# Row maxima of attention scores from half the keys and the difference of the halves, in a kernel that overlaps attention with a scan

## The chip, the core and the metric

The kernel runs on one core of one Trainium2 chip. Its engines work at the same time, each through its own queue in program order: TensorE (PE; matmuls, its weight loads are PEld), VectorE (DVE), ScalarE (ACT), GpSimd (POOL) and SyncE (SP, which issues the DMAs). The metric is the device time of one execution in microseconds; less is better.

## What is computed

Two layers for 16 images of 256 channels and 32 x 32 pixels, seen as 1024 tokens. The first is a transformer block with 4 heads of 32, the second a gated state-space scan over the tokens with 512 inner channels and 64 states. Cut to what matters here:

```python
# layer 0, after a group norm
q, k, v = (qkv[:, :, 0], qkv[:, :, 1], qkv[:, :, 2])
dots = jnp.einsum('bihd,bjhd->bhij', q, k) * scale
attn = jax.nn.softmax(dots, axis=-1)
out = jnp.einsum('bhij,bjhd->bihd', attn, v)
# layer 1, after another group norm
def step(h, inp):
    d_t, B_t, C_t, u_t = inp
    dA = jnp.exp(d_t[..., None] * A)
    h = dA * h + (d_t * u_t)[..., None] * B_t[:, None, :]
    y = jnp.einsum('bdn,bn->bd', h, C_t)
    return (h, y)
```

A softmax is the same whatever is subtracted from a row before the exponential. The kernel subtracts the row's maximum over all 1024 keys, and gets it in a pass of its own.

## The kernel before

**Units and side work.** The scan over one image takes 256 units, one per pair of inner channels (128 partitions are 64 states times 2 channels, the free dimension the 1024 tokens). For unit n the main loop writes, in this order:

- `load(n + 6)` on SP: the channel's input `dub`, 512 KB, into one of 7 buffers; `inputs(n + 4)` on POOL: times B (L911)
- the next part of `outputs` of the eight units before: 32 matmul records into `yb` (L953); ACT copies them off on every second unit (L959); once in eight units 64 more, `turn` (L965), with a copy (L969)
- `scan(n)` on DVE (L928); it needs the decays of unit n and `dub`
- `decay(n + 2)`: two matmuls spread the step sizes into an `a` tile of two banks (L920), an Exp on ACT (L922). There are two `a` tiles, so this waits until `scan(n)` has read its own
- a step of the side work: image b+1's norms, attention and scan inputs, image b-1's gate and store. These are generators; each `yield` gives a share, a share of 1 or more is at least one unit, and the shares are stretched so that the side work of one image fills its 256 units. The number and place of the yields set which unit a step falls in.

A dependency added at the end holds each engine to the program's order. For image 0 the side work runs before the scan starts, alone.

**The row maxima (L412 to L446).** `q4` and `k4` hold the four heads on 32 partitions each. The pass goes over 16 blocks of 64 queries (`c`) and, within each, over the two halves of the keys (`hf`): 32 steps, one yield each. A step computes the scores of four heads against 512 keys: tile `g` of two takes heads 2g and 2g+1, one above the other (`e`), and fills one PSUM bank. The matmul contracts over the head's 32 partitions, so the four heads of a step stand in four row groups of the array. fp32 matmuls stand in the trace as two records each. `maxima()`, at the head of the next step, reduces both tiles over the keys on DVE into one column of `mx` each (L417). At the end `neg` takes the maximum over the two halves and the negative (L446); a transposing matmul and DMAs put it as a 33rd row under the queries, and the later score matmuls then give scores minus maximum.

**PSUM.** Eight banks: `a` has four (`aps`), `yb` one, `accp` one (the attention sums `av`), `mm` two. Beside the scan `psum()` gives the `mm` banks in turn, and `psum3()` goes round `mm, mm, accp`. In the part that runs alone both take from `mm` and the idle `a` tiles through `free_bank`, which hands out an `a` tile in two halves and keeps the second in the list `spare`.

**SBUF tiles the change uses.** `half` (`hwork`): four buffers of 128 x 512 fp32, used by the norms. `ptp` (tag `pt`): four of the same size, used after this pass for the exponentials and for the scan's step sizes.

Of the kernel before, what the change touches and what calls it, by code (L numbers as in the profile page):

```python
# [11 lines left out]
F32 = mybir.dt.float32  # L12
BF16 = mybir.dt.bfloat16
AF = mybir.ActivationFunctionType
ALU = mybir.AluOpType
AX = mybir.AxisListType
# [3 lines left out]
P = 128  # L20
# [3 lines left out]
HL = 512  # L24
NG = 16
HEADS, DH = 4, 32
INNER = HEADS * DH
NJ = L // P
# [22 lines left out]
def attention_then_scan_kernel(  # L51
# [18 lines left out]
    nc = tc.nc  # L70
    B = x.shape[0]

    def pool(name, bufs, **kw):
        return ctx.enter_context(tc.tile_pool(name=name, bufs=bufs, **kw))
# [5 lines left out]
    ptp = pool("ptp", 4)  # L80
    small = pool("small", 2)
# [12 lines left out]
    alone, spare = cycle((mm, aps)), []  # L94

    def bank(src, name):
        return src.tile([P, HL], F32, name=name, tag="mm" if src is mm else "av")

    def free_bank(name):
        if spare:  # L100
            return spare.pop()
        if next(alone) is mm:
            return bank(mm, name)
        both = aps.tile([P, L], F32, name=name, tag="a")
        spare.append(both[:, hs(1)])
        return both[:, hs(0)]

    def psum(name, dims=P):
        return (bank(mm, name) if beside["scan"] else free_bank(name))[:dims]
# [4 lines left out]
    def psum3(name):  # L114
        return bank(next(three), name) if beside["scan"] else free_bank(name)

    def work(name, n=L):
        return wide.tile([P, L + 2 + CONV], F32, name=name, tag="wide")[:, :n]

    def hwork(name):  # L120
        return half.tile([P, HL], F32, name=name, tag="half")

    def hs(h):
        return ts(h, HL)
# [37 lines left out]
    for k in range(ND):  # L162
# [4 lines left out]
        for j in range(2):  # L167
# [3 lines left out]
                start=(j == 0), stop=(j == 1),  # L171
# [195 lines left out]
    def attention_layer(b):  # L367
# [23 lines left out]
        q4, k4 = work("q4"), work("k4")  # L391
# [17 lines left out]

        mx = small.tile([P, 2, 2 * NJ, 2], F32, name="mx", tag="mx")  # L412
        waiting = []

        def maxima():
            for s, g, c, hf in waiting:
                nc.vector.tensor_reduce(mx[:, g, c, hf : hf + 1], s, AX.X, ALU.max)  # L417
            waiting.clear()

        def against(pair, e):  # L420
# [3 lines left out]
        to_space = [  # L424
            partial(spaced, to, src, pair)
            for pair in range(HEADS // 2) for to, src in ((qas, q4), (kas, k4))
        ] + [partial(against, pair, e) for pair in range(HEADS // 2) for e in range(2)]
        for c in range(2 * NJ):
            for hf in range(2):
                maxima()  # L430
                for g in range(2):
                    waiting.append((psum("s_ps"), g, c, hf))
                for h in range(HEADS):
                    g, e = divmod(h, 2)
                    r = ts(h, DH)
                    nc.tensor.matmul(  # L436
                        waiting[g][0][ts(e, 64)], q4[r, ts(c, 64)], k4[r, hs(hf)],
                        start=True, stop=True,
                    )
                if to_space:  # L440
                    to_space.pop(0)()
                yield 1
        maxima()
        del q4, k4, to_space
        neg = small.tile([P, HEADS * NJ], F32, name="neg", tag="neg")
        nc.vector.tensor_reduce(neg, mx.rearrange("p g c k -> p (g c) k"), AX.X, ALU.max, negate=True)  # L446
        ps = psum("neg_ps", HEADS * NJ)[:, :P]
        nc.tensor.matmul(ps, neg, ident, start=True, stop=True)
        yield 1
# [2 lines left out]
        for h in range(HEADS):  # L452
            pair, e = divmod(h, 2)
# [6 lines left out]
        for g in range(2):  # L460
# [3 lines left out]
            for j in range(NJ // 2):  # L464
                for k in range(KC):
                    nc.tensor.matmul(
                        ps[:, j, :], xn[k][:, ts(g * (NJ // 2) + j, P)], wv_s[:, k, :],
                        start=(k == 0), stop=(k == KC - 1),
# [14 lines left out]
        for pair in range(HEADS // 2):  # L483
# [3 lines left out]
            for hf in range(2):  # L487
# [11 lines left out]
                for j in range(NJ):  # L499
                    scores = []  # L500
                    for e in range(2):
                        r = ds(2 * DH * e, DH + 1)
                        s = psum("st_ps")
# [6 lines left out]
                    for s in scores:  # L510
                        pt = ptp.tile([P, HL], F32, name="pt", tag="pt")
# [376 lines left out]
    def load(n):  # L888
        b, k, q, e, i = units[n]
        st = state[b]  # L890
        if (k, q, e, i) == (0, 0, 0, 0):
            bt = hst.tile([P, L], F32, name="bt", tag="bt")
            ct = hst.tile([P, L], F32, name="ct", tag="ct")
            for v, lo in ((bt, 0), (ct, NS)):
                src = st["rows"][lo : lo + NS, :]
                nc.sync.dma_start(v, src.unsqueeze(1).to_broadcast([NS, 2, L]))
            blocks[b] = {"bt": bt, "ct": ct}
        if i == 0:
            pieces = blk.tile([P, HL], BF16, name="pieces", tag="pieces")
            rows = ds(((k * 4 + q) * 2 + e) * 48, 48)  # L900
            for hf in range(2):
                nc.sync.dma_start(pieces[ds(64 * hf, 48)], st["dps"][rows, hs(hf)])
            blocks[b, k, q, e] = pieces
        du = dutp.tile([P, L], F32, name="dub", tag="dub")
        src = st["dus"][ts(k, P)].rearrange("(q j i e) c -> q e i j c", q=4, j=2, i=SLOTS)[q, e, i]
        nc.sync.dma_start(du, src.unsqueeze(0).to_broadcast([NS, 2, L]))
        loaded[n] = du
# [70 lines left out]
    def prepare(b):  # L978
        return chain(first_norm(b), attention_layer(b), scan_inputs(b))
# [15 lines left out]

    AHEAD, LEAD = 6, 4
    beside["scan"] = True
    for n in range(AHEAD):
        load(n)
    for n in range(LEAD):  # L1000
# [5 lines left out]
    for n, (b, k, q, e, i) in enumerate(units):  # L1006
        at = n % UNITS
        if at == 0:
            parts = [prepare(b + 1)] if b + 1 < B else []
            total = steps * len(parts)  # L1010
            if b > 0:
                if b + 1 < B:
                    parts = [
                        first_norm(b + 1, gate_loads(b - 1)), gate_and_store(b - 1),
                        attention_layer(b + 1), scan_inputs(b + 1),
                    ]
                else:
                    parts = [gate_and_store(b - 1)]
                total = total + GATE
            side = chain(*parts)  # L1020
            rate, due = rate_for(total, UNITS - AHEAD - 3), 0.0
# [102 lines left out]
```

## Time and profile before

| | |
|---|---|
| median of 3 runs | 12974.16 us (12973.16 to 13009.8) |
| the profiled execution | 12999.14 us, span 12997.4 us |
| mean granted TensorE clock | 0.799 |
| scan, L928 | 4096 instructions, 9217.0 us busy, 2280 ns each |
| row maxima, L417 | 1023 instructions, 657.5 us busy, 698 ns each |
| score matmuls of that pass, L436 | 4092 records, 823.4 us busy, 617 ns each |
| Exp of the decays, L922 | 4096 instructions, 4463.0 us busy, 1090 ns each |
| the scan's inputs on POOL, L911 | 4096 instructions, 9781.6 us busy, 2410 ns each |

How to read it: the page gives busy time, share of the span and number of instructions of each engine, then groups of instructions: line, engine, operation, tiles written and read, shapes, count, then busy time and mean length of one, then the idle time of the engine just before them and what ended it. The timeline lists instructions in order of time: start, length, engine, line, operation, count. Lengths overlap a little where one instruction starts before the one ahead has drained, so the space an instruction takes in its queue is read from start to start. PEclk is the granted share of the full TensorE clock.

### The profile page before, as it was taken

The page shows a single profiled execution, that of the slowest core. Times are in us where ns is not written, and L with a number is a line of the kernel's source. Part 1 is how long each engine was busy: PE and PEld are TensorE (multiplying, and loading weights), DVE is VectorE, ACT ScalarE, POOL GpSimd, SP SyncE. Part 2 cuts the span into 40 slices and gives each one's busy share as a digit, 9 for nine tenths or more (in the row PEclk, how much of TensorE's full clock was granted, in tenths as well). Part 3 has the DMA queues.
Part 4 walks back from the last instruction along what each step waited for, and adds up shares of the span by engine and source line. Part 5 has one row for each costly group of instructions (what it writes and reads, how often), then busy time and mean ns, then how long its engine had stood idle before and what let it go on. Part 6 is the DMA issues. An engine that isn't in the chain of part 4 may idle for free.

```text
span 12997.4 us, 424123 instructions
## 1 busy us (share of the span) xinstructions
PE 9794.6 (75%) x186800; PEld 5486.9 (42%) x186800; DVE 11576.5 (89%) x7464; ACT 7531.4 (58%) x10421; POOL 10007.5 (77%) x4201
## 2 busy tenths in 40 slices
PE   6676877868778687786878768687786877868777
PEld 2344444444444444444444434444344444444445
DVE  3789999899999899898999999999998998989998
ACT  2465664656646566565665656656565664656654
POOL 0588877878778787787878878787787877878798
PEclk8887977878778797887879878797787978868755
DMA  1467666675666766667666666766667666676676
GB/s 51 166 218 245 206 215 224 221 243 203 212 224 220 241 204 214 230 217 239 207 228 224 217 231 211 241 210 215 225 220 241 209 215 224 224 239 202 224 252 229
DMA packets 1038400, 2820.09 MB, mean 217 GB/s; under 512 B 290370, under 2 KB 368451, under 8 KB 1036548
## 3 DMA queue, kind: packets, MB, share of 16 engines
q1 hardware_dynamic: 1036548, 2792.97, 63.2%
q8 instruction: 1459, 23.90, 0.7%
q14 instruction: 393, 3.22, 0.1%
HBM read 2513.82 MB, written 261.62 MB: 214 GB/s over the span
## 4 chain that ended last, share of the span: by engine, by line
DVE 37%; PE 29%; issue 13%; ACT 10%; DMA 7%; POOL 3%; SPq 1%; DVEq 0%; POOLq 0%; ACTq 0%
DVE h L928 26%; PE yb L953 5%; DVE mx L417 5%; ACT a L922 5%; PE a L920 4%; DMA dub<-dus 4%; PE av L492 3%; POOL dub L911 2%; PE st_ps L504 2%; PE z_ps L640 2%; PE g_ps L689 2%; PE yb L965 1%; PE m_ps L865 1%; DMA xs<-ud 1%; DVE u L675 1%
## 5 line engine op out<-in xcount | busy, mean ns | idle before, releaser
L911 POOL TENSOR_TENSOR dub<-dub,bt 128x1024 f32<-128x1024 f32 x4096 | 9781.6, 2410 | 2841.4 <-DMA dub<-dus 2555.3
L928 DVE TENSOR_TENSOR_SCAN h<-a,dub 128x1024 f32<-128x1024 f32 x4096 | 9217.0, 2280 | 798.1 <-ACT a L922 492.2
L922 ACT ACTIVATE a<-a,acol 128x1024 f32<-128x1024 f32 x4096 | 4463.0, 1090 | 3177.0 <-PE a L920 3112.4
L920 PE MATMUL a<-pieces,pick 48*128 48x512 bf16 x8192 | 1915.4, 458 | 2380.2 <-DVE h L928 2258.4
L953 PEld LDWEIGHTS yb<-h,cd 128*32 128x32 f32 x131072 | 2511.0, 129 | 2808.0 <-issue 1281.3
L953 PE MATMUL yb<-h,cd 128*32 128x64 f32 x131072 | 3283.5, 253 | 472.1 <-ACT y L959 331.8
L920 PEld LDWEIGHTS <-pick 48*128 48x128 bf16 x8192 | 606.0, 95 | 2779.1 <-issue 2368.6
L959 ACT COPY y<-yb 128x256 f32<-128x256 f32 x2048 | 763.0, 373 | 811.5 <-PE yb L953 803.5
L436 PE MATMUL s_ps<-k,q 32*64 32x512 f32 x4092 | 823.4, 617 | 93.4 <-DVE mx L417 93.4
L417 DVE TENSOR_REDUCE mx<-s_ps 128x1 f32<-128x512 f32 x1023 | 657.5, 698 | 20.0 <-PE s_ps L436 20.0
L492 PE MATMUL av<-pt,vv 128*64 128x512 f32 x2048 | 600.1, 666 | 2.8 <-ACT sums L481 1.6
L512 ACT ACTIVATE pt<-st_ps 128x512 f32<-128x512 f32 x1024 | 553.8, 597 | 71.0 <-PE st_ps L504 70.1
L965 PE MATMUL yb<-turn,y 128*32 128x16 f32 x32768 | 590.8, 214 | 4.3 <-issue 3.3
L504 PE MATMUL st_ps<-sp 33*128 33x512 f32 x2048 | 577.8, 640 | 3.3 <-ACT pt L512 3.3
L965 PEld LDWEIGHTS yb<-turn,y 128*32 128x32 f32 x32768 | 573.1, 159 | 5.1 <-issue 3.7
L969 ACT COPY yo<-yb 128x128 f32<-128x128 f32 x512 | 136.0, 266 | 627.0 <-PE yb L965 619.7
L689 PE MATMUL g_ps<-w,xp 128*128 128x256 f32 x1464 | 457.9, 452 | 0.0
L689 PEld LDWEIGHTS g_ps<-w,xp 128*128 128x128 f32 x1464 | 369.1, 326 | 67.1 <-issue 58.1
L436 PEld LDWEIGHTS s_ps<-k,q 32*64 32x64 f32 x4092 | 193.1, 130 | 435.2 <-DVE mx L417 417.0
L675 DVE SCALAR_TENSOR_TENSOR u<-up,cwh,u 128x1024 f32<-128x1024 f32 x192 | 305.1, 1589 | 27.9 <-ACT u L667 27.7
L865 PE MATMUL m_ps<-w,xs 128*128 128x256 f32 x1024 | 317.7, 460 | 11.8 <-POOL xs L840 11.8
L865 PEld LDWEIGHTS m_ps<-w,xs 128*128 128x128 f32 x1024 | 262.2, 328 | 57.6 <-issue 26.0
(177 smaller groups left out, 6805.3 us busy)
## 6 DMA issues: line engine op xcount, KB each, us to landing
dub<-dus SPq DMA_DIRECT2D x4096, 512.0 KB
dps<-pc SPq DMA_DIRECT2D x384, 128.0 KB
pieces<-dps SPq DMA_DIRECT2D x1024, 48.0 KB
xs<-in_x_dram SPq DMA_DIRECT2D x64, 512.0 KB
xs<-kept SPq DMA_DIRECT2D x64, 512.0 KB
zs<-z SPq DMA_DIRECT2D x64, 512.0 KB
ud<-u SPq DMA_DIRECT2D x64, 512.0 KB
dus<-du SPq DMA_DIRECT2D x64, 512.0 KB
```

What stands on the lines that cost most here:

```text
L417: nc.vector.tensor_reduce(mx[:, g, c, hf : hf + 1], s, AX.X, ALU.max)
L436: nc.tensor.matmul(waiting[g][0][ts(e, 64)], q4[r, ts(c, 64)], k4[r, hs(hf)], start=True, stop=True,)
L492: nc.tensor.matmul(av[ts(e, 2 * DH)], vv[j // (NJ // 2)][:, j % (NJ // 2), 2 * pair + e, :], pts[e], start=(j == 0), stop=(j == NJ - 1),)
L504: nc.tensor.matmul(s, ka[r, ts(j, P)], qa[r, hs(hf)], start=True, stop=True)
L689: nc.tensor.matmul(ps[:, ts(q, C)], xp[k][:, ds(first + t, P, 4)], wg_s[:, k, t, :], start=(k == 0 and t == 0), stop=False,)
L911: nc.gpsimd.tensor_tensor(v, v, blocks[units[n][0]]["bt"], ALU.mult)
L920: nc.tensor.matmul(a[:, hs(hf)], w, pieces[r], start=True, stop=True)
L922: nc.scalar.activation(a, a, AF.Exp, scale=acol[:, at : at + 1])
L928: nc.vector.tensor_tensor_scan(now["h", e][:, i, :], decays.pop(n), loaded.pop(n), 0.0, ALU.mult, ALU.add)
L953: nc.tensor.matmul(yb[ts(g, 32), ts(s, 64)], cd[:, at // 16, ts(c, 32)], hbuf[:, :, at : at + 8], start=(c == 0), stop=(c == 1),)
L959: nc.scalar.copy(y2[:, r], yb[:, :256])
L965: nc.tensor.matmul(some[ts(r, 32), x], y2[:, r, x:256:8], turn[:, x], start=True, stop=True)
```

## The change

The maximum of two halves is written as max(s0, s1) = max(s0 - s1, 0) + s1. The difference of the two halves' scores is the score against the difference of the keys, `kd` = first half of `k4` minus second half, made once per image on DVE (512 columns, a `half` buffer).

A step now takes one block of queries and one pair of heads `g`, where it took one half of the keys and all heads; there are 32 steps and yields as before. It fills two PSUM tiles from `psum3`: the two heads against `kd`, then the same two heads against the second half of the keys. In the same step ACT writes the Relu of the first tile into `over`, a `pt` buffer in SBUF. A step later one DVE instruction adds the second tile to `over`, writes the sum back, and takes the maximum along the row into a column of `mx`. `mx` has one column per block and head pair, and `neg` is its negative. Before the scan starts the list `spare` is cleared.

```diff
-        mx = small.tile([P, 2, 2 * NJ, 2], F32, name="mx", tag="mx")
+        mx = small.tile([P, 2 * 2 * NJ], F32, name="mx", tag="mx")
+        kd = hwork("kd")
+        nc.vector.tensor_tensor(kd, k4[:, hs(0)], k4[:, hs(1)], ALU.subtract)
         waiting = []
 
         def maxima():
-            for s, g, c, hf in waiting:
-                nc.vector.tensor_reduce(mx[:, g, c, hf : hf + 1], s, AX.X, ALU.max)
+            for s, r, at in waiting:
+                nc.vector.tensor_tensor_reduce(
+                    r, s, r, 1.0, -3.0e38, ALU.add, ALU.max, mx[:, at : at + 1]
+                )
             waiting.clear()
...
         for c in range(2 * NJ):
-            for hf in range(2):
+            for g in range(2):
                 maxima()
-                for g in range(2):
-                    waiting.append((psum("s_ps"), g, c, hf))
-                for h in range(HEADS):
-                    g, e = divmod(h, 2)
-                    r = ts(h, DH)
-                    nc.tensor.matmul(
-                        waiting[g][0][ts(e, 64)], q4[r, ts(c, 64)], k4[r, hs(hf)],
-                        start=True, stop=True,
-                    )
+                pair = []
+                for keys in (kd, k4[:, hs(1)]):
+                    s = psum3("s_ps")
+                    for e in range(2):
+                        r = ts(2 * g + e, DH)
+                        nc.tensor.matmul(
+                            s[ts(e, 64)], q4[r, ts(c, 64)], keys[r], start=True, stop=True
+                        )
+                    pair.append(s)
+                over = ptp.tile([P, HL], F32, name="over", tag="pt")
+                nc.scalar.activation(over, pair[0], AF.Relu)
+                waiting.append((pair[1], over, g * 2 * NJ + c))
                 if to_space:
                     to_space.pop(0)()
                 yield 1
         maxima()
-        del q4, k4, to_space
+        del q4, k4, to_space, kd, pair, s, keys, over
         neg = small.tile([P, HEADS * NJ], F32, name="neg", tag="neg")
-        nc.vector.tensor_reduce(neg, mx.rearrange("p g c k -> p (g c) k"), AX.X, ALU.max, negate=True)
+        nc.vector.tensor_scalar(neg, mx, -1.0, None, ALU.mult)
...
     beside["scan"] = True
+    spare.clear()
```

`tensor_tensor_reduce` is one instruction: out = (in0 + in1) * 1.0, and its last argument gets the maximum of that and of -3.0e38.

## The prediction

> **What bounds the kernel now.** I read the page first: engine totals, to see who is nearly full.
>
> ```profile
> PE 9794.6 (75%) x186800; PEld 5486.9 (42%) x186800; DVE 11576.5 (89%) x7464; ACT 7531.4 (58%) x10421; POOL 10007.5 (77%) x4201
> ```
>
> VectorE (DVE) leads, but the 89% is a mean over stages. The change touches one: the row maxima of the scores, lines 412 to 446. In the starts of line 417 this stage stands once per batch element, 105.25 us long from its first reduction to the end of its last. In fifteen elements (540.3 to 645.5 us is the first) it runs beside the scan of the element before; once, at 75.7 to 129.8 us, it runs alone, before the scan starts. Second view: busy time in the stretch 2158 to 2264 us, one such stage.
>
> ```profile
> core 0: us, PE busy (x) PEld busy (x) DVE busy (x) ACT busy (x) POOL busy (x), PEclk, DMA share, GB/s
> 2158.00:2264.00 106.00, 86.51 (x1600) 37.27 (x1592) 105.65 (x95) 41.66 (x52) 75.18 (x32) 1.00 0.50 174
> ```
>
> DVE is busy for 105.65 of 106.00 us, at a full TensorE clock, with ScalarE (ACT) under 40%. Third view, its groups:
>
> ```profile
> L911 POOL TENSOR_TENSOR dub<-dub,bt 128x1024 f32<-128x1024 f32 x32 | 75.2, 2351 | 30.5 <-DMA dub<-dus 23.4 <-DVE mx L417 7.1
> L928 DVE TENSOR_TENSOR_SCAN h<-a,dub 128x1024 f32<-128x1024 f32 x32 | 73.6, 2301 | 0.7 <-ACT a L922 0.7
> L417 DVE TENSOR_REDUCE mx<-s_ps 128x1 f32<-128x512 f32 x63 | 40.5, 695 | 0.3 <-PE s_ps L436 0.3
> ```
>
> DVE does one scan and two reductions per unit and waits 1.0 us in all. Fourth view, the timeline of one unit:
>
> ```profile
> 2195.94 1.28 DVE L417 TENSOR_REDUCE mx<-s_ps 128x1 f32<-128x512 f32 x2
> ...
> 2196.09 0.39 PE L920 MATMUL a<-pieces,pick 48*128 48x512 bf16 x2 [0.54 <-DVE h L928]
> ...
> 2196.68 1.67 PE L436 MATMUL s_ps<-k,q 32*64 32x512 f32 x8 [0.19 <-DVE mx L417]
> 2197.12 2.29 DVE L928 TENSOR_TENSOR_SCAN h<-a,dub 128x1024 f32<-128x1024 f32 x1
> ...
> 2198.28 0.65 PE L953 MATMUL yb<-h,cd 128*32 128x64 f32 x32
> ...
> 2199.32 0.68 DVE L417 TENSOR_REDUCE mx<-s_ps 128x1 f32<-128x512 f32 x1
> ```
>
> From 2195.94 to 2199.32 is 3.38 us: the pair of reductions occupies 1.18 us start to start (to 2197.12), the scan 2.20. TensorE (PE) waits twice in it: 0.54 us for the scan, 0.19 for a reduction. The score matmuls come in eight records, two passes for each of four heads.
>
> **The TensorE order that the change brings has a twin.** The stage of z_ps runs four full passes of 512 columns in a row, beside the same scan and output work. Its timeline:
>
> ```profile
> 3355.78 0.65 PE L953 MATMUL yb<-h,cd 128*32 128x64 f32 x32
> ...
> 3356.25 1.13 PE L965 MATMUL yb<-turn,y 128*32 128x16 f32 x64
> ...
> 3357.31 0.39 PE L920 MATMUL a<-pieces,pick 48*128 48x512 bf16 x2
> ...
> 3357.63 1.98 PE L640 MATMUL z_ps<-xp,w 128*128 128x512 f32 x4
> ...
> 3358.76 0.66 DVE L630 SCALAR_TENSOR_TENSOR z<-z_t,z_ps 128x512 f32<-128x512 f32 x1
> 3359.34 2.28 DVE L928 TENSOR_TENSOR_SCAN h<-a,dub 128x1024 f32<-128x1024 f32 x1
> ...
> 3359.55 0.65 PE L953 MATMUL yb<-h,cd 128*32 128x64 f32 x32
> ...
> 3360.13 0.39 PE L920 MATMUL a<-pieces,pick 48*128 48x512 bf16 x2
> ```
>
> TensorE has no gap: decay to z_ps 0.32, z_ps to yb 1.92, yb to the next decay 0.58: 2.82 us. Where turn (L965) falls in, once in eight units, yb to decay is 1.53, 0.95 more. A DVE step that reads one PSUM and one SBUF tensor costs 0.58 start to start (3358.76 to 3359.34).
>
> [...] The trace agrees for two heads in different rows: their passes start within 0.01 us. The change lets two matmuls in a row use the same rows and columns of the array[...]. [...] the 128 Relus of line 766 come behind Exps and there is no table load on that line. [...] 1.00 in this stage, 0.67 at 3600 to 3757 us, where TensorE is busy for 107 of 157 us.
>
> **The change part by part, per unit of the stage.**
>
> DVE: two reductions (1.18) go; one fused add-max over 128x512 comes. No row shows it. From below, line 630's 0.58: one pass over the same two operand places. From above, the scan's rate, which also feeds each result back: 2.20 us for 1024 elements, so 1.13 for 512 with the same overhead. I take 0.60, since a running maximum is what the reduction already does[...]. Scan 2.20 plus 0.60: DVE needs 2.80.
>
> ACT: one Relu from PSUM to SBUF. The nearest row is pt (L512), 597 ns. ACT has 41.66 of 106 us in use, or 1.3 of 3.38 per unit; with the Relu 1.9 of about 2.9. It stands behind the unit's Exp (1.09) and before the next yb copy. Exp ends about 1.5 us after the decay matmul starts; the difference tile is ready at 0.32 + 0.43 + 0.6 = 1.4; so the Relu runs from 1.5 to 2.1 and the next Exp isn't due before 2.8 + 0.4. Hidden. If its cover went, it would cost at most 0.6.
>
> TensorE: the number of matmuls and columns stays. Before, a step held four heads, in four row groups: in the timeline alone 1.67 us, of which 0.6 is the wait for the second bank. After, a step holds two heads, first against the differences kd, then against the second half, in the same two row groups and columns. The two heads overlap; the two key sets can't. So four passes in a row, as in z_ps: 1.92. This is dearer than before by 0.3 to 0.9, but the waits of 0.54 and 0.19 go. The third bank (mm, mm, accp) sees to that: a tile takes the bank of the tile three before, which ACT or DVE read a step earlier. TensorE needs 0.32 + 1.92 + 0.58 = 2.82 per unit, plus 0.95 / 8 = 0.12 for turn, which DVE at 2.80 leaves no slack to absorb: 2.94.
>
> The loop across the engines: decay to end of the second key set 0.32 + 1.44 + 0.59 = 2.35; add-max from 2.4 to 3.0; then the scan, over at 5.3, and the decay two units on. That is 5.35 for two units, under 5.88. The add-max is queued before the next scan and the scan before the decay; so a late Relu or matmul would hold the scan, but has 0.5 us for two units to spare.
>
> GpSimd: 2.35 per unit, under 2.94. DMA: one 512 KB load per unit is 178 GB/s at this pace; other stages move 259. Both are covered, and no DMA changes place on SP's queue.
>
> So per unit 3.38 - 2.94 = 0.44, times 32 units, times 15 stages: 211 us gained.
>
> Costs: kd is one subtraction per element, 0.58 on DVE, behind which the first scores wait; decay's 0.32 covers some, so 0.3 to 0.6, with 15 stages about 7. The final reduction becomes a multiply on 32 elements: nothing (220 ns before). In the stage that runs alone a step takes 54.1 / 32 = 1.69 us; four passes at 0.43 are 1.72 at full clock and 1.89 at the 0.91 it has there, so plus 1 to 6: I take 4. Clearing the spare bank costs no instruction. The cycle over three banks now enters later stages at another place; unknown sign, I allow 20 us each way.
>
> Sum: 211 - 7 - 4 = 200 us less. The profiled execution took 12999.14 us (span 12997.4), so 12799 for one like it. The median of the runs shown is 12974.16, 25 lower; I predict for it: 12775.
>
> **Rivals.**
> (a) The forecast: TensorE becomes the bound at 2.94. Chance 0.67.
> (b) The key sets overlap after all, or drain faster, and DVE sets the pace at 2.80: 0.58 x 480 - 11 = 267 less, 12707. Against it: the same rows and columns of the array. 0.08.
> (c) The fused operation runs at the scan's rate, 1.13. DVE then needs 3.33; 0.05 x 480 - 11 = 13 less, 12961, no change. For it: no row prices it, and the scan is the one DVE operation here with feedback over two operands. Up to about 0.70 its price is hidden behind TensorE; at 0.90 the pace is 3.11 and the time 12855. In all 0.17, of which half still gains over 0.3%.
> (d) Slower: the TensorE clock drops in the stage. It now has no slack: at a clock of 0.80, the mean of the run, 2.94 becomes 3.68, which is 0.30 x 480 + 11 = 155 more, 13129. It decides from a clock of about 0.86 down. For it: neighbouring stages run at 0.6 to 0.8. Against: they run so where TensorE idles, and here it will be nearly full. 0.08, with an add-max above 1.25 us taken in.
>
> **How the numbers follow.** The low end, 12715, lies nearly at (b); the high end, 12860, takes an add-max of 0.9. About 0.3% (39 us) is what a measurement of this kernel can tell from no change. Faster: (a), (b) and half of (c), 0.84; same 0.08; slower 0.08.
>
> **What would show it.** Right: in the stage DVE falls from 100% to about 95%, TensorE is near full, decay no longer waits for the scan, units stand 2.82 apart with one of 3.77 in eight; busy time of the score matmuls rises from 823 to about 1000 us, ACT's by about 306. Wrong: an add-max over 0.7 us, DVE still full, a clock under 1.00, or Relus that wait behind Exps while the add-max waits for them.

## The result, and the profile after

| | before | after |
|---|---|---|
| median of 4 executions | 12977.7 us (12973.16 to 13009.8) | 12880.1 us (12773.48 to 13022.7) |
| all four | 12974.16, 13009.8, 12973.16, 12981.24 | 12813.5, 12946.69, 13022.7, 12773.48 |
| profiled execution: time, span | 12999.14, 12997.4 | 12813.5, 12811.7 |

The ratio is 0.9894, interval 0.9862 to 0.9926; it leaves the execution of 13022.7 us out as disturbed, though the experiments below give that spread a cause in the kernel. So the kernel is faster, by 1.1%, and its executions lie 249 us apart where the four of before lie 37 apart. Two things are to be explained: the gain, and the spread.

The page of the changed kernel, engine totals and the groups of the stage. (The file has more lines now: the scan is L935, the Exp of the decays L929, the decay matmul L927, the output matmul L960, the score matmuls L440, the Relu L445, the add-max L419.)

```profile
PE 9896.8 (77%) x186800; PEld 5493.9 (43%) x186800; DVE 11279.1 (88%) x7480; ACT 7776.4 (61%) x10933; POOL 10022.9 (78%) x4201
...
L440 PE MATMUL s_ps<-kd,q 32*64 32x512 f32 x2044 | 543.5, 618 | 17.1 <-DVE mx L419 9.0
L440 PE MATMUL s_ps<-k,q 32*64 32x512 f32 x2048 | 518.4, 593 | 0.0
...
L419 DVE CUSTOM_DVE_ANT_0 over<-s_ps,over 128x512 f32<-128x512 f32 x512 | 342.9, 671 | 82.3 <-ACT over L445 44.6
...
L445 ACT ACTIVATE over<-s_ps 128x512 f32<-128x512 f32 x511 | 303.3, 594 | 40.0 <-PE s_ps L440 40.0
```

DVE lost 657.5 us of reductions and got 342.9 of add-maxes; ACT got 303.3 of Relus. Now busy time in three stretches: the stage of image 4 (2934.9 to 3026), and the stage of image 3 in two parts. The columns are those of the same view before.

```profile
core 0: us, PE busy (x) PEld busy (x) DVE busy (x) ACT busy (x) POOL busy (x), PEclk, DMA share, GB/s
2139.70:2173.00 33.30, 33.27 (x276) 11.07 (x280) 19.84 (x20) 12.10 (x17) 18.76 (x8) 0.53 0.43 140
2180.00:2196.00 16.00, 15.90 (x252) 6.41 (x252) 15.88 (x19) 9.99 (x14) 11.29 (x6) 1.00 0.50 173
2934.90:3026.00 91.10, 91.10 (x1566) 37.37 (x1566) 89.07 (x94) 56.14 (x83) 74.29 (x32) 1.00 0.64 201
```

TensorE, not DVE, is busy without a break in the stage of image 4. From the first score matmul to the end of the last, undisturbed stages take 91.6 us, against 104.85 before. But image 3's stage begins with 33 us in which TensorE is just as busy, 33.27 of 33.30 us, at a clock of 0.53, while DVE is at 60%. That stage took 107.1 us, longer than every scan stage of before, of which the first took 106.1 and the others 104.85. The timeline of one unit at full clock:

```profile
2983.22 0.67 DVE L419 CUSTOM_DVE_ANT_0 over<-s_ps,over 128x512 f32<-128x512 f32 x1
...
2983.55 0.39 PE L927 MATMUL a<-pieces,pick 48*128 48x512 bf16 x2
2983.81 0.08 DVE L419 DVE_READ_ACCUMULATOR2_ANT mx<- 128x1 f32 x1
2983.81 2.29 DVE L935 TENSOR_TENSOR_SCAN h<-a,dub 128x1024 f32<-128x1024 f32 x1
...
2983.87 1.07 PE L440 MATMUL s_ps<-kd,q 32*64 32x512 f32 x4
...
2984.78 1.02 PE L440 MATMUL s_ps<-k,q 32*64 32x512 f32 x4
...
2985.73 0.65 PE L960 MATMUL yb<-h,cd 128*32 128x64 f32 x32
...
2986.32 0.39 PE L927 MATMUL a<-pieces,pick 48*128 48x512 bf16 x2
```

Decay to decay is 2.77 us, without a wait: 0.32 for the decay, 0.91 for the difference keys, 0.95 for the second half, 0.59 for the output. The two key sets do follow each other. The add-max takes 0.59 before the next scan can start; the read of its accumulator lies beside the scan. DVE's 0.59 and the scan's 2.20 make 2.79, so in an ordinary unit the two engines are nearly tied. The units with turn, 3.57 us, are TensorE's alone.

### The profile page after: what moved, and what is told of

Same layout as the page of the kernel before. It is cut to its first block, busy times and chain, and to the rows that moved or that the text cites. A ratio compares the mean times of both kernels' runs of the same rounds, so it can differ in the third digit from the quotient of the medians.

```text
span 12811.7 us, 424772 instructions
## 1 busy us (share of the span) xinstructions
PE 9896.8 (77%) x186800; PEld 5493.9 (43%) x186800; DVE 11279.1 (88%) x7480; ACT 7776.4 (61%) x10933; POOL 10022.9 (78%) x4201
## 5 line engine op out<-in xcount | busy, mean ns | idle before, releaser
L935 DVE TENSOR_TENSOR_SCAN h<-a,dub 128x1024 f32<-128x1024 f32 x4096 | 9205.6, 2276 | 799.1 <-ACT a L929 475.0
L929 ACT ACTIVATE a<-a,acol 128x1024 f32<-128x1024 f32 x4096 | 4463.7, 1090 | 2870.7 <-PE a L927 2749.6
L960 PEld LDWEIGHTS yb<-h,cd 128*32 128x32 f32 x131072 | 2503.1, 129 | 2812.0 <-issue 1278.9
L960 PE MATMUL yb<-h,cd 128*32 128x64 f32 x131072 | 3274.4, 253 | 479.5 <-ACT y L966 331.3
L927 PE MATMUL a<-pieces,pick 48*128 48x512 bf16 x8192 | 1910.4, 458 | 2158.6 <-DVE h L935 2047.7
L927 PEld LDWEIGHTS <-pick 48*128 48x128 bf16 x8192 | 569.6, 95 | 2564.1 <-issue 2156.1
L440 PE MATMUL s_ps<-kd,q 32*64 32x512 f32 x2044 | 543.5, 618 | 17.1 <-DVE mx L419 9.0
L440 PE MATMUL s_ps<-k,q 32*64 32x512 f32 x2048 | 518.4, 593 | 0.0
L419 DVE CUSTOM_DVE_ANT_0 over<-s_ps,over 128x512 f32<-128x512 f32 x512 | 342.9, 671 | 82.3 <-ACT over L445 44.6
L445 ACT ACTIVATE over<-s_ps 128x512 f32<-128x512 f32 x511 | 303.3, 594 | 40.0 <-PE s_ps L440 40.0
```

Of the source, the lines that this page charges most:

```text
L440: nc.tensor.matmul(s[ts(e, 64)], q4[r, ts(c, 64)], keys[r], start=True, stop=True)
L927: nc.tensor.matmul(a[:, hs(hf)], w, pieces[r], start=True, stop=True)
L929: nc.scalar.activation(a, a, AF.Exp, scale=acol[:, at : at + 1])
L935: nc.vector.tensor_tensor_scan(now["h", e][:, i, :], decays.pop(n), loaded.pop(n), 0.0, ALU.mult, ALU.add)
L960: nc.tensor.matmul(yb[ts(g, 32), ts(s, 64)], cd[:, at // 16, ts(c, 32)], hbuf[:, :, at : at + 8], start=(c == 0), stop=(c == 1),)
```

## Experiments

Theory A: the gain is the predicted one, and it is lost in part because TensorE is now the bound and its clock sometimes stays at half in a stage (0.53 over the 33.30 us above). With two row groups of the array at a time it doesn't come back, however busy TensorE looks. Rival B: the half clock comes from TensorE's new wait for the key difference as the stage starts (0.92 us in image 3's, 0.51 in image 4's), and what fills the array doesn't matter. Both are guesses to be tested.

**Four row groups at once.** The difference tile is computed one item ahead. Each step holds kd of one head pair and the second half of the other, so no two of its matmuls share rows.

```diff
+        clip(0, scores(0, kd))
+        for n, (c, g) in enumerate(items):
+            maxima()
+            ahead = scores(n + 1, kd) if n + 1 < len(items) else None
+            s = scores(n, k4[:, hs(1)])
+            if ahead is not None:
+                clip(n + 1, ahead)
+            waiting.append((s, overs.pop(n), g * 2 * NJ + c))
```

> The difference scores are computed one item ahead, so each step holds the difference tile of one head pair and the second-half tile of the other: four row groups of the array at once, same matmuls, Relus and add-maxes. Theory A (two row groups in a row cost TensorE four passes[...]): TensorE needs 0.32 + 1.02 + 0.58 = 1.92 us per unit, DVE sets the pace at 2.79, also in the units with turn (3.57 in the changed kernel), the clock is 1.00 in every one of the fifteen stages; about 12.72 ms, executions within 40 us of each other. Rival B (the pace is DVE's and the half clock comes from TensorE's wait for the key difference at the stage's start): units and stages as in the changed kernel, about 12.80 ms, with a spread of 100 us or more.

Measured: ratio 0.9828, 0.981 to 0.9847; median 12747.4 us, 27 over theory A's 12.72 ms, five executions from 12741.55 to 12790.02. Every stage beside the scan at clock 1.00, 87.4 to 88.4 us long. Busy time in one:

```profile
core 0: us, PE busy (x) PEld busy (x) DVE busy (x) ACT busy (x) POOL busy (x), PEclk, DMA share, GB/s
2894.00:2980.00 86.00, 65.77 (x1564) 31.17 (x1556) 86.00 (x92) 56.14 (x82) 71.00 (x31) 1.00 0.64 205
```

TensorE has a quarter of the time free, DVE none. Units are 2.79 us, also those with turn, as theory A has it. The number of matmuls is the same; only their neighbours changed. The spread of 48 us also fits: the wait for kd is still there, 1.35 us in one stage, and did no harm. The pace is settled by this run. The half clock isn't: most waits here are the 0.51 us that did no harm in the changed kernel either.

**The key difference made earlier.** k is projected before q, and kd subtracted one step before the scores.

```diff
-        for i, (t, scale) in enumerate(((q4, DH**-0.5), (k4, 1.0))):
+        for i, t, scale in ((1, k4, 1.0), (0, q4, DH**-0.5)):
...
+                if i == 0 and hf == 0:
+                    kd = hwork("kd")
+                    nc.vector.tensor_tensor(kd, k4[:, hs(0)], k4[:, hs(1)], ALU.subtract)
```

> The changed kernel with k projected before q and the key difference made one step before the scores, so that TensorE doesn't wait for it at the start of the stage. Theory A: about 1.3 us less per stage, 20 us in all, and stages at half clock still occur, so executions still differ by 100 us or more. Rival B: no stage at half clock, about 12.75 ms, executions within 40 us of each other.

Measured: ratio 0.9858, 0.9839 to 0.9878; four executions from 12759.52 to 12816.33; no stage at half clock in its trace, and the executions lie within 57 us. In the stages this is rival B's side, though the median, 12803.5, is some 50 us over B's figure. But the early difference only moved the wait. In four of the fifteen entries a decay waited 1.22 to 1.43 us for a scan that stood behind the early kd, and the clock fell to half for 3.4 us just before the scores. What ran then was the projection of q. The entry of image 2, where kd took 2.78 us beside a POOL instruction and not the 0.69 it took alone in the changed kernel's entry of image 4:

```profile
1342.58 0.39 PE L928 MATMUL a<-pieces,pick 48*128 48x512 bf16 x2 [1.34 <-DVE h L936]
1342.90 3.29 PE L404 MATMUL qk_ps<-xn,w 128*128 128x512 f32 x4
```

In the changed kernel's trace four such passes took 1.98 us at full clock (from 2931.48 us). They use the whole array, 128 x 128, and the clock was full again 0.2 to 0.5 us before the first score matmul. So in these four entries the clock fell after a wait of 1.22 to 1.43 us and was back after matmuls over the whole array. That the wait made it fall and these matmuls brought it back is a guess.

**Two banks for three.**

```diff
-                    s = psum3("s_ps")
+                    s = psum("s_ps")
```

> The changed kernel with its score tiles on the two mm banks instead of three. If the third bank is what ends TensorE's waits, a unit of the stage goes from 2.79 to about 3.2 us and the time up by some 200 us. If not (the second-half scores are due 0.96 us after the step begins, when the add-max of the step before is over), a unit stays at 2.79 and the time within the spread of the changed kernel.

Measured: ratio 0.987, 0.9833 to 0.9906; six executions from 12733.58 to 12981.39. Units are 2.79 us. The third bank is worth nothing here. Its profiled execution, 12882.38 us, caught what the changed kernel's had only shown for 34 us. Timeline of TensorE as the stage of image 7 starts, then busy time inside that stage:

```profile
5255.70 0.39 PE L927 MATMUL a<-pieces,pick 48*128 48x512 bf16 x2
5258.77 1.32 PE L440 MATMUL s_ps<-kd,q 32*64 32x512 f32 x4 [2.68 <-DVE kd L414]
```

```profile
core 0: us, PE busy (x) PEld busy (x) DVE busy (x) ACT busy (x) POOL busy (x), PEclk, DMA share, GB/s
5300.00:5425.00 125.00, 125.00 (x1168) 43.05 (x1166) 68.89 (x70) 45.69 (x63) 55.91 (x24) 0.50 0.30 104
```

This stage waited 2.68 us for kd where the other thirteen stages from image 2 on waited 0.51. Its clock fell to half within the first microseconds and stayed there: 125 us of unbroken TensorE work at 0.50. It took 166.7 us, 75 more than its sisters. A unit is 5.16 us.

**The kernel before with the new matmul order alone.**

```diff
-            for hf in range(2):
+            for g in range(2):
                 maxima()
...
+                for hf in range(2):
+                    s = psum("s_ps")
+                    for e in range(2):
+                        r = ts(2 * g + e, DH)
...
+                    waiting.append((s, g, c, hf))
```

> The kernel before, with the order of its score matmuls alone changed: a step takes one head pair against both halves of the keys (two row groups, as in the changed kernel) and not four heads against one half. No key difference, no Relu, reductions as before. Theory A: at full clock TensorE needs 2.79 of DVE's 3.38 us, so undisturbed stages keep their 3.38; but the clock can now stay at half in a stage, where a unit takes about 5.2; time from 12.97 ms up, by up to 57 us for each stage at half clock. Rival B: there is no key difference to wait for, so clock 1.00 in each stage and 12.97 ms.

Measured: ratio 1.0013, 1.0004 to 1.0022. Scan stages at clock 1.00, units 3.38. So two row groups alone didn't start it beside the scan here. In the first part, which runs alone and where TensorE waits for DVE's reductions, 31 of 68.3 us were at half clock; before, with four row groups, it was 10 of 54.5. Each spell ended after 3.4 us in both. In that part of the changed kernel the steps of the two head pairs overlap (1.48 us a step, where its two key sets take 0.91 and 0.95 one after the other), so by my estimate four row groups stream at times in this kernel too. Against the early-kd kernel, which has the same matmul order and no wait right before the scores, this also nearly isolates the replaced reductions: 12998.2 to 12803.5 us, 195 us, with the subtraction and the third bank in it.

Theory A2, a guess from these: after a wait at the stage's start (2.68 us in the two-bank kernel) the clock falls, and with two row groups at a time it then doesn't come back. Two kernels test both halves with a longer wait.

**The wait lengthened, with two and with four row groups.** Both have this edit, on the changed kernel and on the one with four row groups:

```diff
-        nc.vector.tensor_tensor(kd, k4[:, hs(0)], k4[:, hs(1)], ALU.subtract)
+        for _ in range(6):
+            nc.vector.tensor_tensor(kd, k4[:, hs(0)], k4[:, hs(1)], ALU.subtract)
```

> The changed kernel with the key difference computed six times over, so that TensorE waits some 2.9 us longer at the start of each stage; the stage itself is as in the changed kernel. Theory A2 (a wait of TensorE at the start lets its clock fall to half[...]): most of the fifteen stages begin at half clock, with units of 5.16 us until something lifts it, up to 75 us each; 13.1 to 13.9 ms. Rival C (half clock comes at random, whatever the wait): only the wait is paid, 15 x 2.9 = 44 us, about 12.85 ms with the spread of the changed kernel.

> The same six-fold key difference in the kernel with four row groups per step. Theory A2: the clock may be at half as a stage begins, but four row groups bring it back within a few units; 12.75 + 0.04 = 12.79 ms, units at 2.79 in the rest of the stage. If the wait alone decides, stages stay at half as in the other kernel with this wait.

Measured with two: ratio 1.0781, 1.0759 to 1.0802; 14019.0 us, above the 13.1 to 13.9 ms expected, since all but one stage stayed at half and the wait was longer. Fourteen of fifteen stages stood at half clock from the start to the end or nearly so, 165.6 to 167.4 us each; one came free half-way, 127.4 us. With four: ratio 0.993, 0.9904 to 0.9956; 12911.1 us, 7 to 9 us at half clock in each stage, then 1.00. Busy time, first of one stage with two groups; then, with four, of the later part of a stage (upper row) and of its first 9 us (lower row):

```profile
3183.40:3350.70 167.30, 167.25 (x1566) 57.75 (x1566) 92.47 (x94) 59.48 (x82) 72.64 (x31) 0.50 0.31 109
```

```profile
2950.00:3030.00 80.00, 61.19 (x1476) 29.19 (x1470) 80.00 (x88) 52.75 (x77) 64.38 (x28) 1.00 0.58 200
2941.00:2950.00 9.00, 9.00 (x92) 3.24 (x96) 6.70 (x7) 3.43 (x6) 2.36 (x1) 0.50 0.40 124
```

TensorE is fully busy in both half-clock stretches, 167.25 of 167.30 us and 9.00 of 9.00. Its score matmuls work in two row groups at a time in the first and in four in the second, and only the second came free. The wait was longer than I had reckoned, 8.18 us at the stage of 3183 us, not 2.9 more than 0.51: the six subtractions took 8.36 us there, since those that ran beside a POOL instruction took up to 2.71 each. That explains most of why the kernel with four groups came 120 us over its expectation: its unit with the wait is 12.6 us, 7.7 longer, and the two units behind it 2.5 longer in all, 10 us for each of 15 stages, of which the expectation had 2.9.

**Both repairs.**

> Both repairs: four row groups per step, and the key difference made a step before the scores. Theory A2: no stage at half clock, units of 2.79 throughout, no wait at the start: 12.75 ms less about 20 us, 12.73 ms, executions within 50 us. If the early difference only moves the wait to another place: 12.75 ms as without it.

Measured: ratio 0.981, 0.9787 to 0.9833; median 12759.4 us, 12740.56 to 12774.95. All stages at 1.00. The stage with its two entry units is 1 to 2 us shorter than with four groups alone, but the total isn't: the intervals of the two ratios overlap. It is as good a kernel as the one with four groups, not a shown improvement on it. Both beat the kernel before and the changed one, whose intervals lie apart from theirs.

**What about the row groups matters?** With 128 queries of one head in a tile, two row groups work over all columns: as many cells as four groups over half of the columns, with half the matmuls.

```diff
-            for e in range(2):
-                r = ts(2 * g + e, DH)
-                nc.tensor.matmul(s[ts(e, 64)], q4[r, ts(c, 64)], keys[r], start=True, stop=True)
+            nc.tensor.matmul(s, q4[r, ts(j, P)], keys[r], start=True, stop=True)
```

> What brings the clock back: the share of the array in use, or the number of matmul instructions? A tile now holds 128 queries of one head (32 rows x 128 columns of the array, one matmul) where it held 64 queries of two heads (two matmuls). The difference tile is of the next head, so two row groups over all columns work at once: as much of the array as with four row groups of 64 columns, with half as many matmuls, four records per step as against eight in every other kernel. The six-fold wait at the start is kept. If the share in use decides: about 8 us at half clock as a stage begins, then 1.00 and units of 2.79, 12.91 ms. If the number of instructions (or of row groups) decides: half clock through most stages, as with two row groups, 13 to 14 ms.

Measured: 13287.4 us in one execution (before, on the same chip: 12992.3). Clock 0.50 to 0.55 in every stage, though the two matmuls start within 0.01 us of each other. So an equal share of cells, with a unit of 3.55 us at half clock against 3.47 with four groups, didn't bring it back. It left the number of instructions or the row groups. Two more kernels raise the number by cutting each score matmul in two of 256 keys, in this kernel and in the changed one, both with the long wait:

```diff
+            for i in range(2):
+                t = ts(i, HL // 2)
+                nc.tensor.matmul(s[:, t], q4[r, ts(j, P)], keys[r, t], start=True, stop=True)
```

> The kernel with tiles of one head and 128 queries, its matmuls cut in two halves of 256 keys: eight records per step again, as with four row groups, the same columns streamed and the same two row groups at a time. If the number of matmul instructions brings the clock back: 1.00 after some 8 us of a stage, units of 2.79, 12.91 ms. If it is the row groups that stream at once: half clock stays, units of 3.5 to 3.6 us and more, 13.3 ms.

> The changed kernel with the six-fold wait, its score matmuls cut in two halves of 256 keys: sixteen records per step, two row groups at a time, four passes as before. If the number of instructions brings the clock back: stages at 1.00 after some 10 us, 12.9 ms. If the row groups at once do: half clock in most stages and 14.0 ms as with uncut matmuls.

Measured: 13265.6 and 13961.4 us, one execution each (before: 13001.3). With as many records as the four-group kernel the wide one stayed at 0.50 to 0.59; with twice as many the other stood at 0.50 in twelve of fifteen stages. Busy time in a stage of the wide kernel, of its cut form, and of the changed kernel cut:

```profile
3030.00:3140.00 110.00, 110.00 (x1371) 47.07 (x1362) 87.85 (x93) 56.97 (x78) 69.52 (x30) 0.50 0.47 153
```

```profile
3080.00:3110.00 30.00, 30.00 (x406) 18.35 (x402) 23.82 (x25) 15.23 (x21) 19.45 (x9) 0.50 0.46 151
```

```profile
1480.00:1600.00 120.00, 120.00 (x1305) 66.25 (x1307) 65.49 (x67) 43.61 (x60) 53.89 (x23) 0.50 0.31 107
```

What sets the kernel that came free in some 8 us apart from those that didn't is that its score matmuls stream in four row groups at once, not two (in a step of the four-group kernel the passes against kd start at 2940.81 us and those against the second half at 2940.82). Why that counts, no experiment here shows. Several row groups weren't enough by themselves in the trace of before: while the attention of image 0 ran alone, TensorE stood at half clock without a gap for 27.30 us.

```profile
139.40:166.70 27.30, 27.30 (x58) 5.96 (x58) 0.00 (x0) 7.87 (x15) 0.00 (x0) 0.50 0.03 11
```

Its matmuls run two heads at a time there, `av` with all 128 rows and `st_ps` with 33 rows for each head, more than one row group. A few stages with cut matmuls came free early (37.5 us at half in one), so more instructions may help a little.

## The prediction, point by point

**Time.** Predicted 12775 us, range 12715 to 12860. The lowest execution is 12773, the profiled one 12813.5, the median 12880, above the range; the ratio of 0.9894 on 12977.7 gives 12840. Direction and mechanism held; two of the four executions lost most or all of the gain. That 12840 lies in the range is in part luck: the high end had been set for an add-max of 0.9 us, and what used up the room is the clock.

**The sum, against the two profiled executions.** Over the unit with the entry and the 32 units after it, an undisturbed image went from 111.8 to about 98.2 us, 13.6 less, where the prediction had 14.1 less 0.5. For the fifteen images the sum of these stretches fell from 1675.4 to 1487.8 us: 187.6, nearly the difference of the spans (185.7). Had image 3's stretch taken 98.2 and not 113.5 us, it would be 203, where the prediction's terms for the stages, 211 and 7, give 204.

**The bound passes from DVE to TensorE.** Right, though by little outside the units with turn. Predicted 2.82 per unit and 3.77 with turn, measured 2.79 and 3.57; DVE at 97.8%, predicted about 95%. The twin in the z_ps stage had given the pace. The score matmuls' busy time went from 823 to 977 us, predicted about 1000. The four-group kernel shows the other side: with the rows shared no more, DVE holds it at 2.79, the 2.80 of rival (b); the time is 12747 us, where (b) had 12707.

**The add-max.** Right: 0.60 taken, 0.59 before the next scan starts, and the read of the accumulator hidden. Rival (c) is out.

**The Relu.** Right: hidden, 594 ns, ACT at 62% of the stage.

**The third bank.** Wrong: I gave it the credit for TensorE's waits going. With two banks the pace is the same. The add-max of the step before is over when the second key set is due.

**The key difference.** Mis-sized: 0.3 to 0.6 us per stage. DVE's timeline at one entry:

```profile
2927.62 4.47 DVE L935 TENSOR_TENSOR_SCAN h<-a,dub 128x1024 f32<-128x1024 f32 x2 [0.30 <-POOL dub L918]
2934.13 0.69 DVE L414 TENSOR_TENSOR kd<-k 128x512 f32<-128x512 f32 x1 [2.04 <-ACT k L407]
2934.74 2.28 DVE L935 TENSOR_TENSOR_SCAN h<-a,dub 128x1024 f32<-128x1024 f32 x1
```

I counted the subtraction and not what it waits for: the copy of k's last half, written one step earlier, is not ready, and DVE stands idle for 2.04 us with the next scan queued behind. That unit grew by 1.95 us. The better pace of the units, 2.89 on average (28 of 2.79, 4 of 3.57) where 2.94 was predicted, made up for it. That the two errors cancel is luck.

**The part that runs alone.** Predicted 4 us longer, it was 7 shorter (54.5 to 47.4 us). Four passes in a row were priced at 0.43 each; but steps alternate between the head pairs, and with nothing between them the passes of neighbouring steps overlap: a step takes 1.48 us on average there, less than the 0.91 and 0.95 of its two key sets.

**The clock.** This is the step that failed. Rival (d), with 0.08, was ruled down by "they run so where TensorE idles, and here it will be nearly full". I took busy time for what decides the clock, an estimate from two stretches of the trace of before: 1.00 at 2158 to 2264 us, where TensorE is busy for 86.51 of 106 us, and 0.67 at 3600 to 3757, where it is busy for 106.79 of 157. Other stretches differ: 125.00 of 125.00 us busy at 0.50 in the two-bank kernel, and 27.30 of 27.30 in the kernel before, where I could have seen it. Beside the scan, with two row groups at once, being busy mostly didn't lift the clock: fourteen of the fifteen stages with the long wait stayed at half to the end or nearly so, 165.6 to 167.4 us each. So the half clock is not paid for with 2.94 turning into 3.68 in every stage, as (d) had it, but all or nothing: 2.79 or 5.16 for as long as it lasts. Whether it comes may be chance of the wait at the entry, which differs from stage to stage (0.92 us before the slow one of the changed kernel, 0.51 before most others); that is a guess. In the kernel before, with four row groups and DVE at 3.38 us a unit, half clock might have cost less. None of its fifteen scan stages had any, so this is not shown.

That the executions of 12946.69 and 13022.7 us had two or three such stages fits their mean clocks (0.787 and 0.781, against 0.798 in the one of 12773.48 and 0.796 in the profiled one) and their times at 75 us per stage. No trace of them exists, so for these two it is inferred.

## What to carry to other kernels

When a change makes TensorE the bound of a stage, read at what clock it runs there. Busy time didn't tell it here: 125.00 of 125.00 us busy at 0.50 in the two-bank kernel, 91.10 of 91.10 at 1.00 in the changed one. Put matmuls of small contraction side by side in different row groups, even if that means computing one of them a step ahead: here it cost nothing that the runs show, and took the ratio from 0.9894 to 0.9828 and the spread from 249 to 48 us. And price an instruction that is moved to the head of a queue with the wait for its own input: 0.6 us of subtraction held DVE for 2.7.

## What the runs showed of the hardware

- With two row groups at a time TensorE stood at half clock through nearly whole stages, fully busy. Two banks, image 7: a wait of 2.68 us, a stage of 166.7 us, 125.00 of 125.00 us busy at 0.50. The long wait: fourteen of fifteen stages of 165.6 to 167.4 us; in the one that waited 8.18 us, 167.25 of 167.30 us busy at 0.50. The long wait with four row groups at once: half clock for 7 to 9 us at the start of a stage, then 1.00.
- In the changed kernel twelve of the fifteen stages beside the scan began with a wait of 0.51 us and one with 0.19, all at clock 1.00. The stage that waited 0.92 us fell to half for 34 us; the one that waited 0.90 stayed at 1.00. With four row groups a stage that waited 1.35 us stayed at 1.00.
- The add-max with two inputs took 671 ns for 512 columns in the changed kernel, plus a separate read of the accumulator of 84 ns; the plain reduction of one input took 698 ns in the kernel before.
